# Merging two quarter-array products of an attention step into one of 64 rows and 128 columns

## The chip, the cores and the metric

The kernel runs on one core of one Trainium2 chip, in float32 throughout. The metric is the device time of one execution in microseconds (us), as the median of several runs. Beside it stands one profiled execution, from which every duration below is taken.

## The reference

x has the shape (2, 2048, 256). Four blocks follow one another, each adding its result to x after a layer norm: a gated linear scan, a feed-forward block with ternary weights, an attention of higher order, and the same feed-forward block again. The change lies in the attention. With 16 heads, 64 wide, q, k and v are projections of the normalised x, and per head, step by step in time:

```python
def step(carry, qkv):
    S_K, C_QV, G = carry
    q_t, k_t, v_t = qkv
    k_C = einsum('bhk,bhkv->bhv', k_t, C_QV)
    G = G + k_t[..., :, None] * k_C[..., None, :]
    S_K = S_K + k_t[..., :, None] * k_t[..., None, :]
    C_QV = C_QV + q_t[..., :, None] * v_t[..., None, :]
    S_C = einsum('bhkj,bhjv->bhkv', S_K, C_QV)
    o_t = einsum('bhk,bhkv->bhv', q_t, S_C - G)
    return (S_K, C_QV, G), o_t
...
out = outs.transpose(1, 0, 2, 3).reshape(b, t, H * DV) @ W_o
```

This is the same as two causal linear attentions in a row: u = sum over earlier and present k of k (k.q), and o = sum over earlier and present v of v (u.q).

## The kernel before

The kernel first runs the scan and the first feed-forward block ("front"), then the attention, into which the start of the second feed-forward block is woven, then the rest of that block. The order of the instructions on TensorE (PE), VectorE (DVE), ScalarE (ACT) and GpSimd (POOL) is written out by hand: what the code calls first comes first on its engine. SyncE (SP) issues the transfers, in order.

The attention has 32 steps, `s` = 0 to 31: 16 pieces of 128 rows in time, for each of the two batches in turn (even steps are called `first` in the code). A step's 128 rows are two chunks of 64, `c` = 0 and 1; the 16 heads are 8 pairs, `p`, and the two of a pair, `h`, lie in the two halves of the 128 partitions. So every product of the attention proper has 64 rows and 64 columns, and uses one quarter of TensorE's array. The weights are always the first operand, `lhsT`; the second, `rhs`, streams.

Per step, in the order of the instructions on TensorE:

- `inter(s, "S", "uT")` (line 1068) multiplies q with S, the sums of k kT over the earlier chunks, and leaves the result in two PSUM banks `huT`. In the first two steps, for which no earlier sums exist, it leaves out the half of c = 0.
- `products(s, "kT", "p1")` (L1051) multiplies q with k of its own chunk, into two banks `hp`; VectorE multiplies them with the causal mask into `p1` (L1057).
- `outward(s - 3, 1)` (L1129) is part of the output projection of an earlier step, five full-size products.
- `intra(s, "S", "kN", "p1", "uT")` (L1082) multiplies p1 with k and adds to the banks `huT`; `intra(s - 2, "M", ...)` (L1082) does the like for the second attention, with v.
- ScalarE evicts `huT` to `uT` in three copies (`evict`, L1093 and L1095).
- Then come projections of a later piece: q, k and v are each made by seven products (`Seven`, L992 and L997, banks `hqT_X` and so on), whose results ScalarE and VectorE copy and add.
- `update(s + 1, "kN", "kN", "S")` (L1108) adds the next step's k kT to the sums: VectorE writes S after each of its two chunks (L1118). `update(s - 1, "uN", "vN", "M")` is the like for the second attention, with sums M.
- `inter(s - 1, "M", "oT")` and `products(s - 1, "uT", "p2")` (L1068, L1051) are the second attention's products with q, and `outward(s - 2, 0)` starts the next output projection.

k is needed transposed (`kT`). This is done beside TensorE: VectorE transposes squares of 32 (`keys_out`, L235), SyncE writes them to memory and reads them back in another order into `rawkT` (`turn_rows`, four transfers), and ScalarE copies them into place (`turn_end`, L1148). `uN` is made from `uT` in the same way.

The eight PSUM banks are three rings: four banks `ps`, two `uT`, two `oT`. A bank is written again in turn, once what it held has been read. The product `hp` takes two `ps` banks, `huT` the two `uT` banks; the projections take `ps` for their bank Y, and `uT` or `oT` for X and Z.

Of the kernel before, what the change touches and what calls it, by code (L numbers as in the profile page):

```python
# [17 lines left out]
FP = mybir.dt.float32  # L18
AF = mybir.ActivationFunctionType
ALU = mybir.AluOpType  # L20
AX = mybir.AxisListType

P = 128
B, T, D = 2, 2048, 256
# [3 lines left out]
H, DK = 16, 64  # L28
NPR = H * DK // P
# [5 lines left out]
CH = 64  # L35
SQ = 32
NQ = P // SQ
# [6 lines left out]
def kernel(  # L44
# [15 lines left out]
    nc = tc.nc  # L60
# [7 lines left out]
    def bank(shape, name, tag="ps"):  # L68

        ring = rings[tag]  # L70
        ring.append(ring.pop(0))
        return psum_pool.tile(shape, FP, tag=f"bank{ring[-1]}", bufs=1, name=name)
# [67 lines left out]
    for c in range(2):  # L140
        r = slice(c * CH, (c + 1) * CH)
# [10 lines left out]
    def norm_stats(pool, cs, rms=False, bias=False, between=None):  # L152

        n, g0 = len(cs), cs[0]
        st = pool.tile([P, BC, 6], FP, tag="st", name=f"st{g0}")
        mv = pool.tile([P, BC, 2], FP, tag="mv", name=f"mv{g0}")
        rs = pool.tile([P, BC], FP, tag="rs", name=f"rs{g0}")
        for c, g in enumerate(cs):
            nc.vector.bn_stats(st[:, c, :], x_sb[:, g, :])  # L159
            nc.vector.bn_aggr(mv[:, c, :], st[:, c, :])  # L160
            if between and c == n // 2 - 1:
                between()
        mean, var = mv[:, :n, 0], mv[:, :n, 1]
        r = rs[:, :n]
        if rms:


            nc.vector.tensor_scalar(r, var, LN_EPS, RMS_EPS * RMS_EPS / D, ALU.add, ALU.mult)
            nc.vector.tensor_tensor(r, r, var, ALU.max)  # L169
        else:  # L170
            nc.gpsimd.tensor_scalar_add(r, var, LN_EPS)
        nc.gpsimd.tensor_tensor(r, r, mhalf[:, :n], ALU.pow)  # L172
        nb = None
        if bias:
            nb = pool.tile([P, BC], FP, tag="nb", name=f"nb{g0}")
            nc.gpsimd.tensor_tensor(nb[:, :n], mean, r, ALU.mult)
            nc.gpsimd.tensor_scalar_mul(nb[:, :n], nb[:, :n], -1.0)  # L177
        return mv, rs, nb
# [748 lines left out]
    def attention(keep, pool, state, last):  # L927
        halves = [slice(0, CH), slice(CH, P)]

        def feats(h, p):  # L930

            return slice(p * P + h * DK, p * P + (h + 1) * DK)
# [6 lines left out]
        def pair_sums(n):  # L939

            x = pairs[n]
            S = pool.tile([P, 4, P], FP, tag="S", bufs=1, name=f"S{n}")
            l, r = slice(0, P), slice(P, 2 * P)
            x11, x12, x21, x22 = x[:, 0, l], x[:, 1, l], x[:, 0, r], x[:, 1, r]
            for o, a, b_, op in (
                (S[:, 0, :], x21, x22, ALU.add), (S[:, 1, :], S[:, 0, :], x11, ALU.subtract),
                (S[:, 2, :], x11, x21, ALU.subtract), (S[:, 3, :], x12, S[:, 1, :], ALU.subtract),
            ):
                nc.gpsimd.tensor_tensor(o, a, b_, op)  # L949
            pairs[n] = x, S  # L950
# [89 lines left out]

        mask8 = mask2.unsqueeze(1).to_broadcast([P, NPR, CH])

        def products(s, left, nm):


            b, n = steps[s]
            banks = [bank([P, NPR, CH], f"h{nm}{b}_{n}_{h}") for h in range(2)]
            for p in range(NPR):
                for c in range(2):
                    for h in range(2):  # L1050
                        nc.tensor.matmul(  # L1051
                            banks[h][halves[c], p, :], lhsT=d[s][left][halves[h], p, halves[c]],
                            rhs=d[s]["qT"][halves[h], p, halves[c]], start=True, stop=True,
                        )
            d[s][nm] = pool.tile([P, 2, NPR, CH], FP, tag=nm, bufs=1, name=f"{nm}{b}_{n}")
            for h in range(2):
                nc.vector.tensor_tensor(d[s][nm][:, h], banks[h], mask8, ALU.mult)  # L1057

        def inter(s, sums, nm):

            b, n = steps[s]
            banks = [bank([P, NPR, CH], f"h{nm}{b}_{n}_{c}", nm) for c in range(2)]
            for p in range(NPR):
                for c in range(2):
                    if d[s][sums][c] is None:
                        continue
                    for h in range(2):
                        nc.tensor.matmul(  # L1068
                            banks[c][halves[h ^ c], p, :], lhsT=d[s][sums][c][halves[h], p, :],
                            rhs=d[s]["qT"][halves[h], p, halves[c]],  # L1070
                            start=(p == 0), stop=False, skip_group_check=True,
                        )
            d[s][nm + "b"] = banks

        def intra(s, sums, nat, pm, nm):

            b, n = steps[s]
            banks = d[s][nm + "b"]
            for p in range(NPR):
                for c in range(2):  # L1080
                    for h in range(2):
                        nc.tensor.matmul(  # L1082
                            banks[c][halves[h ^ c], p, :], lhsT=d[s][nat][halves[c], feats(h, p)],
                            rhs=d[s][pm][halves[c], h, p, :],
                            start=(d[s][sums][c] is None and p == 0), stop=True,
                            skip_group_check=True,
                        )

        def evict(s, nm, copy=act):
            b, n = steps[s]  # L1090
            banks = d[s][nm + "b"]
            t = pool.tile([P, NPR, P], FP, tag=nm, bufs=2 if nm == "uT" else 1, name=f"{nm}{b}_{n}")
            copy(t[:, :, halves[0]], banks[0])  # L1093
            for h in range(2):
                copy(t[halves[h], :, halves[1]], banks[1][halves[h ^ 1], :, :])  # L1095
            d[s][nm] = t

        def update(s, left, right, sums):


            b, n = steps[s]
            prev = before.get((b, sums))
            last = n == CPB - 1
            banks = [bank([P, NPR, DK], f"h{sums}{b}_{n}_{c}") for c in range(1 if last else 2)]
            for p in range(NPR):
                for c in range(len(banks)):
                    for h in range(2):
                        nc.tensor.matmul(  # L1108
                            banks[c][halves[h], p, :], lhsT=d[s][left][halves[c], feats(h, p)],
                            rhs=d[s][right][halves[c], feats(h, p)], start=True, stop=True,  # L1110
                        )
            d[s][sums] = [prev]
            for c in range(len(banks)):
                t = state.tile([P, NPR, DK], FP, tag=f"{sums}{b}", bufs=3, name=f"{sums}{b}_{n}_{c}")
                if prev is None:
                    nc.vector.tensor_copy(t, banks[c])
                else:
                    nc.vector.tensor_tensor(t, prev, banks[c], ALU.add)  # L1118
                d[s][sums].append(t)
                prev = t  # L1120
            before[b, sums] = prev
# [19 lines left out]
        def turn_rows(s, nm):  # L1141
            d[s]["r" + nm] = squares_in(pool, nm + "{}_{}".format(*steps[s]), d[s]["d" + nm], 2)

        def turn_end(s, nm):

            b, n = steps[s]
            t = pool.tile([P, NPR, P], FP, tag=nm, bufs=1, name=f"{nm}{b}_{n}")
            act(t, d[s]["r" + nm].rearrange("p t q -> p q t"))  # L1148
            d[s][nm] = t
# [18 lines left out]

        NS = len(steps)
        pair_sums(0)  # L1170
        stats = norm_stats(norm_pool, pair(1), bias=True)
        k, q, v = Seven(0, "kN", "oT"), Seven(0, "qT", "uT"), Seven(0, "vN", "oT")
        k.go(2, 1, 0, 5)
# [2 lines left out]
        q.go(1)  # L1176
        k.go(3)
        keys_out(0)
        turn_rows(0, "kT")
        k.go(7)  # L1180
        q.go(0, 5, 6)
        xn = norm_rows(norm_pool, pair(1), stats)
# [7 lines left out]
        q.go(4)  # L1190
        update(0, "kN", "kN", "S")
        v.go(6)
        turn_end(0, "kT")
        v.go(3, 7)
        for s in range(NS):
            first, n = s % 2 == 0, s // 2
            more = n + 1 < CPB
            inter(s, "S", "uT")
            products(s, "kT", "p1")
            if first and n + 2 < CPB:  # L1200
                stats = norm_stats(norm_pool, pair(n + 2), bias=True)
            elif s == NS - 4:
# [20 lines left out]
            last.part()  # L1223
            if s >= 3:
                outward(s - 3, 1)
            intra(s, "S", "kN", "p1", "uT")
            if s >= 2:
                intra(s - 2, "M", "vN", "p2", "oT")
            if s + 1 < NS:
                turn_rows(s + 1, "kT")  # L1230
            evict(s, "uT")
            if not more:
                evict(s - 2, "oT", act if first else dve)
                last.begin(first)
# [48 lines left out]
            if s == NS - 1:  # L1283
                update(s, "uN", "vN", "M")
            if first and not more:
                turn_end(s + 1, "kT")
            if not more:
                fill(2)
            elif first:
# [9 lines left out]
            if first and s > 0:  # L1299
                units_out(s)  # L1300
            if more:
                turn_end(s + 1, "kT")
            if s >= 1:
                inter(s - 1, "M", "oT")
                products(s - 1, "uT", "p2")
# [47 lines left out]
    def pair(n):  # L1353
        return [b * CPB + n for b in range(B)]
# [101 lines left out]
    with tc.tile_pool(name="keep", bufs=3) as keep_pool:  # L1456
# [10 lines left out]
        with tc.tile_pool(name="ffn2", bufs=1) as ffn_pool, tc.manual_schedule(engines=by_hand):  # L1467
            tags = ("uT", "ps", "oT")
            steps = last.outs
# [61 lines left out]
```

## Time and profile before

| | |
|---|---|
| time, median of 3 runs | 1206.71 us (1206.5 to 1206.82) |
| the profiled execution's own time | 1205.26 us |
| its span in the profile | 1203.4 us |
| TensorE matmuls busy | 1194.4 us |
| TensorE weight loads busy (they overlap the matmuls) | 972.1 us |
| VectorE busy | 816.0 us |
| ScalarE busy | 619.9 us |
| GpSimd busy | 252.5 us |
| steps of the attention in the span | from about 319 to about 1005 us |

The profile's page lists the busy time of each engine, the chain of waits that ended last, and the groups of instructions by line. The timeline gives instructions in order of time, neighbours of one kind merged to one line with a count. An f32 matrix product of the code appears as two weight loads and two matmuls; a matmul that reads f32 is thus counted twice. Groups of matmuls overlap in the timeline by the time that the last of a group takes to leave the array.

### The profile page before, as it was taken

How to read it: one execution, taken by the hardware profiler on the slowest of the kernel's cores; microseconds unless marked ns; L12 is line 12 of the kernel's file. 1: busy time of each engine (PE TensorE's matmuls, PEld its weight loads, DVE VectorE, ACT ScalarE, POOL GpSimd, SP SyncE). 2: the span in 40 equal slices, each digit the busy share in tenths (PEclk: the TensorE clock that was granted, in tenths of full speed). 3: DMA queues.
4: the chain of work that ended last, by engine and by line, in shares of the span. 5: the costliest groups of instructions: out<-in, count | busy, mean ns of one | idle time of the engine just before them, and what ended most of it. 6: DMA issues, size and time to landing. Idle time of an engine off the chain costs nothing.

```text
span 1203.4 us, 46653 instructions
## 1 busy us (share of the span) xinstructions
PE 1194.4 (99%) x21156; PEld 972.1 (81%) x21156; DVE 816.0 (68%) x1323; ACT 619.9 (52%) x983; POOL 252.5 (21%) x382
## 2 busy tenths in 40 slices
PE   9999999999999999999999999999999999999998
PEld 7599999999677777777777777777777889999998
DVE  7967877875667667666666756766666655677764
ACT  5366775543554554555545455455455452555442
POOL 3765235461110110110011011011001102222330
PEclk9999999999999999999999999999999999999999
DMA  9111111120244234234324323323433631212111
GB/s 336 71 62 36 36 36 35 37 71 1 89 130 138 92 108 125 91 108 142 117 84 133 125 84 125 126 92 107 130 105 101 183 100 46 71 71 71 54 53 36
DMA packets 80550, 112.99 MB, mean 94 GB/s; under 512 B 8288, under 2 KB 65504, under 8 KB 80096
## 3 DMA queue, kind: packets, MB, share of 16 engines
q1 hardware_dynamic: 77872, 106.07, 26.6%
q10 hardware_dynamic: 2448, 3.93, 1.1%
q8 instruction: 166, 2.72, 1.0%
q14 instruction: 32, 0.26, 0.1%
q0 software_dynamic: 32, 0.00, 0.0%
HBM read 58.59 MB, written 51.38 MB: 91 GB/s over the span
## 4 chain that ended last, share of the span: by engine, by line
PE 98%; DVE 1%; issue 0%; DMA 0%; ACT 0%; POOL 0%; ACTq 0%; DVEq 0%; POOLq 0%
PE hy L1129 10%; PE ox L632 10%; PE hx L539 9%; PE hkN_X L997 5%; PE hp L1051 5%; PE hqT_X L992 5%; PE hvN_X L997 5%; PE oz L632 5%; PE hz L539 5%; PE pq L339 3%; PE huT L1082 3%; PE hS L1108 3%; PE huT L1068 3%; PE hoT L1068 3%; PE hoT L1082 3%; PE hM L1108 3%
## 5 line engine op out<-in xcount | busy, mean ns | idle before, releaser
L1057 DVE TENSOR_TENSOR p<-hp,mask 128x512 f32<-128x512 f32 x128 | 82.1, 682 | 83.2 <-PE hp L1051 83.2
L949 POOL TENSOR_TENSOR S<-xnT 128x128 f32<-128x128 f32 x32 | 14.8, 463 | 531.4 <-ACT xnT L283 513.7
L1129 PE MATMUL hy<-wo,oT 128*128 128x256 f32 x512 | 123.7, 385 | 0.0
L191 ACT ACTIVATE xn<-x_sb,nb,rs 128x256 f32<-128x256 f32 x124 | 65.8, 592 | 85.4 <-POOL nb L177 83.5
L1129 PEld LDWEIGHTS hy<-wo,oT 128*128 128x128 f32 x512 | 93.6, 190 | 19.0 <-issue 6.7
L551 ACT ACTIVATE hT<-hT,b_sb 128x256 f32<-128x256 f32 x192 | 85.4, 501 | 34.6 <-DVE hT L583 31.7
L1093 ACT COPY uT<-huT 128x512 f32<-128x512 f32 x32 | 18.8, 586 | 129.3 <-PE huT L1082 129.3
L1118 DVE TENSOR_TENSOR S<-S,hS 128x512 f32<-128x512 f32 x60 | 41.2, 687 | 43.0 <-PE hS L1108 39.9
L235 DVE STREAM_TRANSPOSE sqkT<-kN 128x1024 f32<-128x1024 f32 x32 | 65.9, 2059 | 1.3 <-ACT kN L1028 1.2
L1148 ACT COPY kT<-rawkT 128x1024 f32<-128x1024 f32 x32 | 66.7, 2084 | 0.0
L235 DVE STREAM_TRANSPOSE squN<-uT 128x1024 f32<-128x1024 f32 x31 | 63.6, 2051 | 4.1 <-ACT uT L1095 3.7
L1148 ACT COPY uN<-rawuN 128x1024 f32<-128x1024 f32 x31 | 64.6, 2085 | 1.7 <-DMA rawuN<-dsquN 1.3
L516 POOL TENSOR_TENSOR xT<-xnT 128x256 f32<-128x256 f32 x15 | 16.9, 1124 | 179.2 <-ACT xnT L283 118.5
L159 DVE BATCH_NORM_STATS2 st<-x_sb 128x6 f32<-128x256 f32 x128 | 51.4, 403 | 2.3 <-DMA x_sb<-in_x_dram 2.3
L1108 PEld LDWEIGHTS hS<-kN 64*64 64x64 f32 x1984 | 32.7, 134 | 23.2 <-issue 23.1
L1002 DVE TENSOR_TENSOR kN<-kN,hkN_Y 128x512 f32<-128x512 f32 x16 | 11.0, 686 | 58.1 <-ACT kN L1011 58.1
L1028 ACT COPY vN<-hvN_X 128x512 f32<-128x512 f32 x16 | 9.4, 587 | 78.8 <-PE hvN_X L997 78.8
L172 POOL TENSOR_TENSOR rs<-rs,mhalf 128x2 f32<-128x2 f32 (+1 forms) x43 | 38.9, 904 | 33.1 <-DVE rs L169 30.3
L640 DVE TENSOR_TENSOR x_sb<-x_sb,ox 128x256 f32<-128x256 f32 x63 | 26.0, 413 | 28.8 <-PE ox L632 28.8
L622 DVE TENSOR_TENSOR hS<-hT 128x512 f32<-128x512 f32 x62 | 41.2, 686 | 5.6 <-ACT hT L551 5.6
L1118 DVE TENSOR_TENSOR M<-M,hM 128x512 f32<-128x512 f32 x60 | 41.0, 684 | 4.6 <-PE hM L1108 1.4
L1082 PEld LDWEIGHTS huT<-p,kN 64*64 64x64 f32 x2048 | 33.4, 134 | 12.8 <-issue 7.0
(303 smaller groups left out, 3031.1 us busy)
## 6 DMA issues: line engine op xcount, KB each, us to landing
dsqkT<-sqkT SPq DMA_DIRECT2D x32, 512.0 KB, 3.6
rawkT<-dsqkT SPq DMA_DIRECT2D x128, 128.0 KB, 3.0
dsquN<-squN SPq DMA_DIRECT2D x31, 512.0 KB, 3.4
rawuN<-dsquN SPq DMA_DIRECT2D x124, 128.0 KB, 3.1
out_dram<-x_sb SPq DMA_DIRECT2D x15, 256.0 KB, 2.2
x_sb<-in_x_dram SPq DMA_DIRECT2D x7, 512.0 KB, 8.9
dsqxn<-sqxn SPq DMA_DIRECT2D x14, 256.0 KB, 4.0
rawxn<-dsqxn SPq DMA_DIRECT2D x56, 64.0 KB, 2.4
```

The lines of the kernel that those rows point to most:

```text
L235: nc.vector.transpose(to, src)
L539: nc.tensor.matmul(at[a][:, j, :], lhsT=A[:, f * P : (f + 1) * P], rhs=Bm, start=(new and j == 0), stop=True, skip_group_check=True,)
L551: nc.scalar.activation(out, out if src is None else src[:, j, :], AF.Gelu, bias=b1_sb[:, f : f + 1])
L632: nc.tensor.matmul(banks[name][:, c, :], lhsT=A[f // 2][:, f % 2, c * P : (c + 1) * P], rhs=Bm[:, f, :], start=(new and c == 0 and f == 0) ...
L997: nc.tensor.matmul(to, lhsT=self.A[i], rhs=self.B[i], start=new, stop=True, skip_group_check=True)
L1057: nc.vector.tensor_tensor(d[s][nm][:, h], banks[h], mask8, ALU.mult)
L1068: nc.tensor.matmul(banks[c][halves[h ^ c], p, :], lhsT=d[s][sums][c][halves[h], p, :], rhs=d[s]["qT"][halves[h], p, halves[c]], start=(p = ...
L1082: nc.tensor.matmul(banks[c][halves[h ^ c], p, :], lhsT=d[s][nat][halves[c], feats(h, p)], rhs=d[s][pm][halves[c], h, p, :], start=(d[s][su ...
L1108: nc.tensor.matmul(banks[c][halves[h], p, :], lhsT=d[s][left][halves[c], feats(h, p)], rhs=d[s][right][halves[c], feats(h, p)], start=True ...
L1118: nc.vector.tensor_tensor(t, prev, banks[c], ALU.add)
L1129: nc.tensor.matmul(py, lhsT=d[s]["oT"][:, p, :], rhs=wo[:, p, :], start=(p == 0), stop=(p == NPR - 1),)
L1148: act(t, d[s]["r" + nm].rearrange("p t q -> p q t"))
```

## The change

The weights of `inter(s, "S", "uT")` and of `products(s, "kT", "p1")` are laid side by side in one tile `W`, of 9 slots with 2 times 64 columns: in each slot `W[:, p, 0]` holds kT and `W[:, p, 1]` holds S. A product takes 128 neighbouring columns of it. For the lower half of the partitions (h = 0) kT is shifted by one slot, so that its 128 columns are S and then k, and for h = 1 they are k and then S. `wide_products` is thus one product of 64 rows and 128 columns with q where there were two; its result has S q in one half of the partitions and k q in the other, in four banks (two of the ring `uT` for c = 0, two of `ps` for c = 1).

Around it:

- VectorE masks k q in four instructions on 64 partitions, where it had two on 128.
- `wide_intra` adds p1 times k to the half of each bank that holds S q. It now stands behind `intra(s - 2, "M", ...)`, not ahead of it.
- `wide_evict` copies the four half banks to `uT`, where there were three copies.
- `keys_in` reads the transposed k into a buffer with 8 more elements, one element further on for the lower half, and GpSimd clears one element at either end. `keys_end` copies it to the two tiles `W` (c = 0 and 1) in two ScalarE instructions of 9 x 64 elements, where there was one of 1024.
- `update` writes the sums S into `W`. The tiles of c = 0 have three buffers, those of c = 1 one. The sums M get one buffer for c = 0 and three for c = 1, for both batches, where there were three for each batch.
- For the first two steps the sums are set to zero and the products with them are computed.

```diff
+        def wide(c):
+            return state.tile([P, NPR + 1, 2, CH], FP, tag=f"W{c}", bufs=1 if c else 3, name=f"W{c}")
+
+        def wide_products(s):
+            b, n = steps[s]
+            banks = [[bank([P, NPR, CH], f"hu{b}_{n}_{h}{c}", "ps" if c else "uT") for c in range(2)] for h in range(2)]
+            for c in range(2):
+                w = d[s]["W"][c].rearrange("p a two e -> p (a two e)")
+                for p in range(NPR):
+                    for h in range(2):
+                        at = (2 * p + 1 - h) * CH
+                        nc.tensor.matmul(
+                            banks[h][c][:, p, :], lhsT=w[halves[h], at : at + 2 * CH],
+                            rhs=d[s]["qT"][halves[h], p, halves[c]],
+                            start=(p == 0), stop=False, skip_group_check=True,
+                        )
+            d[s]["p1"] = pool.tile([P, 2, NPR, CH], FP, tag="p1", bufs=1, name=f"p1{b}_{n}")
+            for c in range(2):
+                for h in range(2):
+                    other = halves[1 - h]
+                    nc.vector.tensor_tensor(
+                        d[s]["p1"][halves[c], h], banks[h][c][other], mask8[other], ALU.mult
+                    )
+            d[s]["ub"] = banks
+
+        def wide_intra(s):
+            for p in range(NPR):
+                for c in range(2):
+                    for h in range(2):
+                        nc.tensor.matmul(
+                            d[s]["ub"][h][c][halves[h], p, :], lhsT=d[s]["kN"][halves[c], feats(h, p)],
+                            rhs=d[s]["p1"][halves[c], h, p, :],
+                            start=False, stop=True, skip_group_check=True,
+                        )
+
+        def wide_evict(s):
+            b, n = steps[s]
+            t = pool.tile([P, NPR, P], FP, tag="uT", bufs=2, name=f"uT{b}_{n}")
+            for c in range(2):
+                for h in range(2):
+                    act(t[halves[h], :, halves[c]], d[s]["ub"][h][c][halves[h]])
+            d[s]["uT"] = t
+
+        def keys_in(s):
+            dr = d[s]["dkT"]
+            raw = pool.tile([P, NPR * P + 8], FP, tag="raw", bufs=2, name="rawkT{}_{}".format(*steps[s]))
+            nc.gpsimd.memset(raw[halves[0], :1], 0.0)
+            nc.gpsimd.memset(raw[halves[1], NPR * P : NPR * P + 1], 0.0)
+            for b in range(NQ):
+                at = 1 if b < NQ // 2 else 0
+                nc.sync.dma_start(
+                    out=raw[b * SQ : (b + 1) * SQ, at : at + NPR * P].rearrange("i (a c) -> i a c", a=NQ),
+                    in_=dr[:, :, b, :].rearrange("a i c -> i a c"),
+                )
+            d[s]["rkT"] = raw
+
+        def keys_end(s):
+            for c in range(2):
+                r = d[s]["rkT"][:, c * CH * NPR : (c + 1) * CH * NPR]
+                act(
+                    d[s]["W"][c][:, :, 0, :],
+                    bass.AP(tensor=r.tensor, offset=r.offset, ap=[list(r.ap[0]), [1, NPR + 1], [NPR, CH]]),
+                )
...
-                t = state.tile([P, NPR, DK], FP, tag=f"{sums}{b}", bufs=3, name=f"{sums}{b}_{n}_{c}")
+                if sums == "S":
+                    w = wide(1 - c)
+                    if c == 0:
+                        d[s]["W"].append(w)
+                    else:
+                        d[s + B]["W"] = [w]
+                    t = w[:, :NPR, 1, :]
+                else:
+                    t = state.tile([P, NPR, DK], FP, tag=f"M{c}", bufs=3 if c else 1, name=f"M{b}_{n}_{c}")
...
-            inter(s, "S", "uT")
-            products(s, "kT", "p1")
+            wide_products(s)
...
-            intra(s, "S", "kN", "p1", "uT")
             if s >= 2:
                 intra(s - 2, "M", "vN", "p2", "oT")
+            wide_intra(s)
             if s + 1 < NS:
-                turn_rows(s + 1, "kT")
-            evict(s, "uT")
+                keys_in(s + 1)
+            wide_evict(s)
...
-                turn_end(s + 1, "kT")
+                keys_end(s + 1)
```

More of the change, by code (lines that the diff above doesn't have):

```diff
@@ L1170, in attention @@
         pair_sums(0)
+        for s in range(B):
+            w = wide(0)
+            nc.gpsimd.memset(w[:, :NPR, 1, :], 0.0)
+            d[s]["W"] = [w]
         stats = norm_stats(norm_pool, pair(1), bias=True)
@@ L1178, in attention @@
         keys_out(0)
-        turn_rows(0, "kT")
+        keys_in(0)
         k.go(7)
@@ L1192, in attention @@
         v.go(6)
-        turn_end(0, "kT")
+        keys_end(0)
         v.go(3, 7)
@@ L1301, in attention @@
             if more:
-                turn_end(s + 1, "kT")
+                keys_end(s + 1)
             if s >= 1:
```

## The prediction

> **What bounds the kernel now.** I read the page first: the busy times, then the chain of waits. TensorE works in 99% of the span and carries 98% of the chain that ended last, at full clock; every other engine is far below.
>
> ```profile
> span 1203.4 us, 46653 instructions
> ...
> PE 1194.4 (99%) x21156; PEld 972.1 (81%) x21156; DVE 816.0 (68%) x1323; ACT 619.9 (52%) x983; POOL 252.5 (21%) x382
> ...
> PEclk9999999999999999999999999999999999999999
> ...
> PE 98%; DVE 1%; issue 0%; DMA 0%; ACT 0%; POOL 0%; ACTq 0%; DVEq 0%; POOLq 0%
> ```
>
> A busy PE row says only that some matmul was in flight, so what a matmul costs has to come from how often they start. For that I took the timeline of TensorE inside one step of the attention (columns: start, length, engine, line, operation, tiles, shapes, count). The length of a group includes the 0.22 us that its last instruction takes to drain; the distance between the starts of neighbouring groups is what counts.
>
> ```profile
> 724.00 1.05 PE L992 MATMUL hqT_X<-xnT,wq 128*128 128x128 f32 x8
> 724.89 1.02 PE L997 MATMUL hvN_X<-wv,xnT 128*128 128x512 f32 x2
> ...
> 739.03 1.46 PE L1129 MATMUL hy<-wo,oT 128*128 128x256 f32 x6
> 740.42 1.16 PE L1068 MATMUL huT<-qT,S 64*64 64x64 f32 x64
> 741.40 1.11 PE L1051 MATMUL hp<-qT,kT 64*64 64x64 f32 x64
> 742.45 2.43 PE L1129 MATMUL hy<-wo,oT 128*128 128x256 f32 x10
> ```
>
> The two groups that the change merges are L1068 huT (q with the sums) and L1051 hp (q with k). Each has 32 products in the code and 64 instructions here: an f32 product is two passes, each a weight load and a matmul. Both together occupy TensorE from 740.42 to 742.45, 2.03 us, nothing idle between them, in each of 32 steps.
>
> What sets their pace? One place in the trace runs the same kind of product on two quarters only: the last step, where an update makes only half its banks.
>
> ```profile
> 989.86 2.08 PE L1108 MATMUL hM<-vN,uN 64*64 64x64 f32 x64
> ```
>
> 64 instructions on two quarters: 2.08 - 0.22 = 1.86 us, 32 per quarter, 58 ns each. On four quarters: 1.16 - 0.22 = 0.94 us, 16 per quarter, 59 ns each. A quarter takes one pass every 58 to 59 ns whatever the others do; the number of instructions does not set the pace (14.7 ns apart on four quarters, 29 on two).
>
> Last, the groups by line with shapes kept apart (columns: busy us, mean ns of one).
>
> ```profile
> L1051 PE MATMUL hp<-qT,kT 64*64 64x64 f32 x2048 | 36.2, 218 | 0.2 <-issue 0.2
> ...
> L992 PE MATMUL hqT_X<-xnT,wq 128*128 128x128 f32 x128 | 16.9, 275 | 0.0
> ...
> L1051 PEld LDWEIGHTS hp<-qT,kT 64*64 64x64 f32 x2048 | 33.3, 135 | 0.4 <-issue 0.4
> ...
> L992 PEld LDWEIGHTS hqT_X<-xnT,wq_t 128*128 128x128 f32 x128 | 15.5, 191 | 1.6 <-DVE qT L1002 0.5
> ```
>
> A matmul lasts 57 ns longer for 64 more streamed columns (275 - 218), and a load 56 ns longer for 64 more weight columns (191 - 135): both run at about 0.88 ns a column. With 64 and 64 columns, load and stream are equally long and overlap (one pass in 58 ns); with 128 and 128 a pass takes (724.89 - 724.00) / 8 = 111 ns. So today's passes are balanced. Which of the two sets the pace cannot be seen in them, and the change tips the balance.
>
> **The change, part by part.** *The merged product.* It has 32 products of 64 rows, 128 weight columns and 64 streamed columns, 64 instructions, on two halves of the array: 32 passes per half. Each streams 64 columns as before, but loads 128. If the longer of the two sets the pace, a pass costs 111 ns: 32 x 111 = 3.55 us. Before, 2 x 0.94 = 1.88 us. That is +1.67 us a step, on the path, 32 steps: +53.5 us. The first two steps, whose huT has half its products, gain nothing from that: their two quarters take the same time, and the change computes the zero sums too. Bounds for a pass under this reading: 107 ns (128 x 0.83, the slope from 128 to 512 columns, (595 - 275) / 384) to 118 (twice 59): +1.5 to +1.9 us a step, +49 to +61 us. I take 111, the measured row.
>
> [...]
>
> The number of instructions halves. By the rows that is worth nothing: they start 14.7 ns apart on four quarters, and with half as many on two quarters the pace per quarter stays. [...]
>
> *Changes of array shape.* The neighbours of the merged group are full-size matmuls (L1129) as before, and the two products with p stay together. No shape change is added: 0.
>
> *Masks.* Two of 128x512 (L1057, 682 ns each, the pair in 1.29 us) become four of 64x512, which by L1095 on VectorE (two in 1.39 us) last as long: +1.3 us a step, +42 us on VectorE, 816 to 858 of some 1260. Their cover: the first pair can start when the c = 0 half of the product is done, 1.8 us before its end; then the outward part (2.4 us) and the product p2 with v (0.98 us), which the change puts ahead of the product p1 with k, run before p1 is read. The second pair ends 1.5 us after the product, 3.3 us are there. Nothing on the path from the third step on; in the first, without that cover, about 1 us.
>
> *Eviction of uT.* ScalarE's 0.59 + 1.17 us become four of 64x512, 2.34 us. The product p1 with k now comes last, so the eviction starts about 1 us later against what follows. The queued copies behind it shift by up to 1.5 us in odd steps: the copy of rawuN (2.05 us), then the first qT and vN copies, for whose banks the sixth products wait. In odd steps qT's first copy moves from 725.09 to about 726.7 and ends at 727.3; its bank is written again at 727.50. It fits by 0.2 us. In even steps the kN product after next wants the first uT bank, free about 0.7 us after the eviction can begin, with 0.96 us of L997 ahead of it. Without this cover it would cost its 0.6 us a step.
>
> *k's turn.* One ScalarE copy of 1024 elements (2.08 us) becomes two of 576 at the same stride, 2 x 1.17 us: +0.26 us. It ends at 712.7 in the even step that I followed (709.67 + 0.59 + 2.4), where q's product starts at 715.74, and in the odd one at 738.1 against 740.42. The merged product now needs both, where huT needed only the sums, but the margin stays above 2 us. The four rows of k's transfer land 4 bytes off; the first copy of them begins 4 us after they land (703.29 + 3.06 against 710.15): hidden. Two tiny writes on GpSimd now wait for the same buffer as the transfers, and ScalarE's two copies wait for them; what stands behind them on GpSimd, the sums of x, has the 37 us of idle that the timeline shows ahead of it at 740.94. SyncE's order is unchanged. M's first half with one buffer is read and rewritten a step apart, except in the last step: under 1 us.
>
> Waits altogether: I take 0.1 us a step, 3 us. Bounds: -1 (the 1.1 us idle at L1082 now) to +0.5 a step, 16 us, if the shifted copies on ScalarE miss their banks each time.
>
> Sum: +53.5 + 3 = +57 us. The profiled execution took 1205.26 us, span 1203.4 and 1.9 around it; it becomes 1262. The median of the runs is 1.45 above it: 1206.71 + 57 = 1264.
>
> **Rivals.**
>
> *The load keeps up (not slower).* A row half today receives 2 x 64 weight columns in one pass time, as two loads for two quarters side by side (the L1051 group). If one load of 128 columns for 64 rows is as fast, a pass stays at 58.5 ns, the product costs 32 x 58.5 = 1.87 us, and only waits are left: -1 to +16, about 1209. For it: that quarters are fed in parallel, and that the loads of the transposes (L215, 128 columns, one pass) last 141 ns. Against: in every two-pass product of the trace a load of 128 columns lasts 56 ns longer than one of 64. It decides below about 61 ns a pass: at 61, 32 x 2.5 x 32 is 2.6 us, no longer nothing.
>
> *Instructions bind (faster).* If the issue of small products were the limit, half of them would take 0.94 us for the 1.88: -0.94 x 32 = -30 us, 1177 us. Against: the 64 instructions on two quarters took twice as long as on four. It needs a pass in a half at 30 ns.
>
> *No overlap in a half (much slower).* If the two halves, which now share all output columns, cannot load side by side, 64 x 111 = 7.1 us: +5.2 a step, 1374 us. If a half could not load while it streams, 111 + 53 ns a pass: 1316 us. Against: L1051 has quarters above each other in turn and runs as fast as groups on the diagonal.
>
> *It doesn't do what it says:* products stay 64 columns wide. The instructions as built show 128, so I give it no chance of its own.
>
> **How the numbers follow.** Load sets the pace: 0.82; the load keeps up: 0.10; instructions bind: 0.04; no overlap: 0.04. The forecast's own ends are 49 - 1 = +48 and 61 + 16 = +77: 1254 to 1284. That holds nearly all of 0.82, and with it eight in ten; the three others lie outside. A measurement of this kernel tells a change of 0.2%, 2.4 us, from none. The rival at about 1209 splits: 0.01 faster, 0.05 same, 0.04 slower. Faster: 0.04 + 0.01 = 0.05; same 0.05; slower 0.82 + 0.04 + 0.04 = 0.90.
>
> **What would show it.** Right: the merged group's 64 instructions take about 3.6 us between the starts of their neighbours, loads of 64x128 last about 190 ns, and two start every 111 ns; L1068's other use and L1082 keep 0.94 to 0.98; TensorE stays at 99%. Wrong: a pass at 58 ns, or a load at 135; or idle TensorE ahead of the sixth products (qT, vN, kN) that adds up to more than 16 us.

## The result, and the profile after

| | before | after |
|---|---|---|
| median of five runs | 1206.71 us (1205.84 to 1207.13) | 1268.59 us (1262.36 to 1268.67) |
| profiled execution, its span | 1205.26, 1203.4 us | 1268.59, 1266.8 us |

The ratio is 1.0501, with a 95% interval of 1.0486 to 1.0515: 5% slower. The five runs after spread over 6 us, which those before do not. The mean granted TensorE clock goes with it: 0.994 in the three runs at 1268.6, 0.997 at 1264.91, 0.999 at 1262.36. That is the second finding below.

The page of the changed kernel: TensorE is as full as before, with 1984 matmuls fewer and 61 us more.

```profile
span 1266.8 us, 43085 instructions
...
PE 1255.5 (99%) x19172; PEld 1031.4 (81%) x19172; DVE 864.3 (68%) x1387; ACT 643.6 (51%) x1047; POOL 258.6 (20%) x448
...
PEclk9999999999899999999999999999999989999999
```

The timeline of TensorE in one step, the same stretch as was shown before:

```profile
964.81 1.46 PE L1209 MATMUL hy<-wo,oT 128*128 128x256 f32 x6
966.20 3.79 PE L1059 MATMUL hu<-qT,W 64*128 64x64 f32 x64
969.92 2.42 PE L1209 MATMUL hy<-wo,oT 128*128 128x256 f32 x10
```

64 instructions in place of 128, and 969.92 - 966.20 = 3.72 us from neighbour to neighbour in place of 2.03: +1.69 us in each of 32 steps, 54.1 us. Groups by line (busy us, mean ns of one):

```profile
L1059 PE MATMUL hu<-qT,W 64*128 64x64 f32 x2048 | 122.1, 275 | 1.4 <-ACT kN L1028 0.7 <-ACT qT L1028 0.7
L1059 PEld LDWEIGHTS hu<-qT,W 64*128 64x128 f32 x2048 | 117.6, 189 | 12.8 <-issue 9.3 <-ACT kN L1028 1.5 <-ACT qT L1028 0.9
```

A load of 64 rows and 128 columns takes 189 ns, as one of 128 rows and 128 columns did (190), where one of 64 rows and 64 columns took 135: halving the rows makes no difference here, halving the columns does. In the trace the starts in one half lie 111 to 112 ns apart, once the group has begun. A matmul that streams 64 columns is now listed with 275 ns, where it was 218. The profile models the ends of matmuls, so this length is not used here; the starts are.

### The profile page after: what moved, and what is told of

The parts are those of the page before. It is cut to its first block, busy times and chain, and to the rows that moved or that the text cites. A ratio compares the mean times of both kernels' runs of the same rounds, so it can differ in the third digit from the quotient of the medians.

```text
span 1266.8 us, 43085 instructions
## 1 busy us (share of the span) xinstructions
PE 1255.5 (99%) x19172; PEld 1031.4 (81%) x19172; DVE 864.3 (68%) x1387; ACT 643.6 (51%) x1047; POOL 258.6 (20%) x448
## 4 chain that ended last, share of the span: by engine, by line
PE 98%; DVE 1%; issue 0%; ACT 0%; POOL 0%; ACTq 0%; DVEq 0%; POOLq 0%
PE hu L1059 9%; PE hy L1209 9%; PE ox L632 9%; PE hx L539 9%; PE hkN_X L997 5%; PE hqT_X L992 5%; PE hvN_X L997 5%; PE oz L632 4%; PE hz L539 4%; PE pq L339 3%; PE hS L1179 3%; PE hoT L1153 3%; PE hoT L1139 3%; PE hM L1179 3%; PE hu L1078 2%; PE hp L1122 2%
## 5 line engine op out<-in xcount | busy, mean ns | idle before, releaser
L1089 ACT COPY uT<-hu 64x512 f32<-64x512 f32 x128 | 74.3, 580 | 214.4 <-PE hu L1078 212.1
L1068 DVE TENSOR_TENSOR p<-hu,mask 64x512 f32<-64x512 f32 x128 | 88.2, 689 | 73.3 <-PE hu L1059 71.3
L1059 PEld LDWEIGHTS hu<-qT,W 64*128 64x128 f32 x2048 | 117.6, 189 | 12.8 <-issue 9.3
L1059 PE MATMUL hu<-qT,W 64*128 64x64 f32 x2048 | 122.1, 275 | 1.4 <-ACT kN L1028 0.7
L1109 ACT COPY W<-rawkT 128x576 f32<-128x576 f32 x64 | 77.0, 1254 | 0.0
L1198 DVE TENSOR_TENSOR W<-W,hS 128x512 f32<-128x512 f32 x60 | 41.3, 688 | 32.5 <-PE hS L1179 29.3
L1128 DVE TENSOR_TENSOR p<-hp,mask 128x512 f32<-128x512 f32 x64 | 40.9, 680 | 20.3 <-PE hp L1122 20.3
```

Of the source, the lines that this page charges most:

```text
L1059: nc.tensor.matmul(banks[h][c][:, p, :], lhsT=w[halves[h], at : at + 2 * CH], rhs=d[s]["qT"][halves[h], p, halves[c]], start=(p == 0), sto ...
L1068: nc.vector.tensor_tensor(d[s]["p1"][halves[c], h], banks[h][c][other], mask8[other], ALU.mult)
L1089: act(t[halves[h], :, halves[c]], d[s]["ub"][h][c][halves[h]])
L1109: act(d[s]["W"][c][:, :, 0, :], bass.AP(tensor=r.tensor, offset=r.offset, ap=[list(r.ap[0]), [1, NPR + 1], [NPR, CH]]),)
```

## The experiments

Distances between the first products with q of successive steps show where each kernel spends its time, from the profiled execution of each (us; odd and even are the usual values of the middle steps):

| kernel | odd | even | step 0 | step 1 | step 30 |
|---|---|---|---|---|---|
| before | 24.68 | 18.44 | 13.03 | 21.20 | 19.79 |
| after | 26.38 | 20.28 | 15.81 | 26.09 | 25.55 |
| e1_quarters | 24.68 | 18.58 | 14.70 | 21.26 | 24.01 |
| e4_waits | 26.38 | 20.27 | 18.12 | 23.87 | 20.64 |
| e5_waits | 26.38 | 20.28 | 15.06 | 23.87 | 20.64 |
| e6_quarters_order | 24.68 | 18.44 | 14.69 | 21.25 | 19.78 |

In the middle the changed kernel is 1.70 us longer in odd steps and 1.84 in even ones. Steps 0, 1 and 30 carry more, and those are the ones in which TensorE stood idle or its clock fell (a fall costs its step 3.4 us, as is worked out at e4_waits).

**e1_quarters: everything but the merged product.**

```diff
-nc.tensor.matmul(banks[h][c][:, p, :], lhsT=w[halves[h], at : at + 2 * CH], ...)
+for j in range(2):
+    nc.tensor.matmul(banks[h][c][halves[j], p, :],
+                     lhsT=w[halves[h], at + j * CH : at + (j + 1) * CH], ...)
```

> The changed kernel with each merged product split again into two of 64 weight columns, on the two quarters side by side; all the rest of the change (tiles W, four masks, four evictions, two copies of k, the order) stays. Theory (the loads of 128 columns set the pace): the group goes from 3.72 us back to about 2.0 us, so 32 x 1.7 = 54 us less than the changed kernel's 1262 to 1269; 1208 to 1215 us, what is left over 1206.7 being waits and clock dips. Rival (the rest of the change, its masks, evictions and order, carries a large part of the loss): 1225 us or more.

Measured: 1213.4 us (1213.19 to 1216.18), ratio 1.0064 (1.0049 to 1.0079) to 1206.11 of the kernel before beside it. The group is back at 2.02 us:

```profile
745.94 2.09 PE L1060 MATMUL hu<-qT,W 64*64 64x64 f32 x128
747.96 2.42 PE L1210 MATMUL hy<-wo,oT 128*128 128x256 f32 x10
```

Its middle odd steps are those of before and its even ones 0.14 us longer. So the merged product alone makes 1.70 us in every middle step, 54.4 us for 32 of them.

The times differ by less. At the same mean clock of 0.999 the changed kernel took 1262.36 us and e1_quarters 1213.2: 49.2 us. The profiled executions show where the other 5 us are. Five middle steps of e1_quarters (8, 10, 14, 16 and 23) are 0.2 to 1.1 us longer than the usual ones, 3.2 us together; the trace names no reason, and the changed kernel has one such step, of 0.15 us. (The kernel before has four, 11, 24, 25 and 26, 1.7 us together.) In steps 0, 1, 2 and 29 the difference between the two, without the fall of the clock in step 1, is below 1.70 us, by 2.1 us in all. So the 7 us that e1_quarters takes over the kernel before are not what the rest of the change costs in the changed kernel. At clock 0.999 that one is 1262.36 - 1206.71 = 55.7 us longer in all, only 1.3 us more than the 54.4.

**e2_stream128: twice the stream under the same load.**

```diff
-banks[h][c][:, p, :], ..., rhs=d[s]["qT"][halves[h], p, halves[c]],
+two neighbouring slots of banks[h][c], ..., rhs=d[s]["qT"][halves[h], p, :],
```

> The changed kernel with 128 columns of q streamed in each merged product in place of 64 (the sums it makes are not those of the reference). Theory: a load of 128 columns takes as long as a stream of 128, both overlap, a pass stays at 111 ns and the time at 1262 to 1269 us. Rival (in a half, load and stream do not overlap, 64 streamed columns are part of the 111 ns): 53 ns more for each of 1024 passes of a half, 1317 us or more. On the clock: if the half-empty stream is what lets the clock drop, the dips at the start of the attention go away; if idle time alone does, they stay.

Measured: 1266.05 us (1263.89 to 1267.03), ratio 1.0489 (1.0472 to 1.0507). The timeline's group:

```profile
730.58 3.84 PE L1060 MATMUL hu<-qT,W 64*128 64x128 f32 x64
734.35 2.43 PE L1210 MATMUL hy<-wo,oT 128*128 128x256 f32 x10
```

3.77 us against 3.72: twice as many streamed columns for 0.05 us, which go at the start of the group; within it the starts lie 111 to 112 ns apart as before. Stream and load overlap in a half, and in the changed kernel half of the stream's time was empty.

The median is below the changed kernel's 1268.59 because the clock fell less: its mean is 0.997 to 1.0 in these four runs, where three of the changed kernel's five have 0.994. In the profiled run the fall at the start of the attention is gone, that at step 30 is not. That is the first of the two cases that were set down for the clock, though in few runs.

**e3_cols96: fewer columns to load, in the same shape of tile.**

```diff
-banks[h][c][:, p, :], lhsT=w[halves[h], at : at + 2 * CH],
+banks[h][c][:m, p, :], lhsT=w[halves[h], at : at + m],      # m = 128 for p = 0, else 96
...
-d[s]["p1"][halves[c], h], banks[h][c][other], mask8[other], ALU.mult
+d[s]["p1"][halves[c], h], banks[h][c][halves[0]], mask8[halves[0]], ALU.mult
```

> The changed kernel with 96 weight columns in place of 128 in 28 of the 32 merged products of a step (the result is not that of the reference). Theory: a pass goes with its loaded columns, 96 x 0.83 + 5 = 85 ns, 26 ns less for 28 of 32 passes of a half in 32 steps: 23.5 us less than the changed kernel, 1239 to 1245 us. Rival (the shape of the tile, all 128 output columns in use, sets the pace): no difference, 1262 to 1269 us.

Measured: 1238.65 us (1238.45 to 1241.49), ratio 1.0274 (1.0258 to 1.0289). Timeline and loads:

```profile
736.05 3.04 PE L1060 MATMUL hu<-qT,W 64*128 64x64 f32 x64
739.02 2.43 PE L1210 MATMUL hy<-wo,oT 128*128 128x256 f32 x10
```

```profile
L1060 PEld LDWEIGHTS hu<-qT,W 64*96 64x96 f32 x1792 | 81.5, 162 | 0.0
```

The group takes 2.97 us, the starts in a half lie 85 ns apart where 96 columns are loaded, and the whole is 23.7 us less than the changed kernel's 1262.36 (the run at clock 0.999, as the three lower ones here), 0.35 us under the expected range. A pass follows the columns of its load: 58, 85 and 112 ns for 64, 96 and 128. A matmul here multiplies with just the columns that its load brings, 96 too, so no run tells the load itself from the use of as many columns; what is shown is that the weight columns set the pace and, by e2_stream128, the streamed ones do not.

**e7_swapped: the wide operand streams.**

```diff
-lhsT=w[halves[h], at : at + 2 * CH], rhs=d[s]["qT"][halves[h], p, halves[c]]      # two halves
+lhsT=d[s]["qT"][halves[h], p, halves[c]], rhs=w[c][halves[h], at : at + 2 * CH]   # four quarters
```

> e1_quarters with the merged product turned round: the 64 columns of q are the weights, the 128 columns of S and k stream, 32 products on the four quarters (the sums come out turned and later steps use them as they lie, so the result is not that of the reference). Theory (a pass costs the longer of load and stream; 0.83 ns a column plus 5 ns; quarters run side by side): 16 passes of 111 ns per quarter, 1.78 us, about 1.95 us between the neighbours' starts against 2.02 in e1_quarters and 3.72 in the changed kernel; 1210 to 1213 us. Rival (the halving of the instructions helps once the load is short): 1.0 us, 1180 us.

Measured: 1209.01 us (1207.23 to 1211.98), ratio 1.0027 (1.0018 to 1.0037), 1 us under the theory's 1210 to 1213.

```profile
742.60 1.98 PE L1059 MATMUL hu<-W,qT 64*64 64x128 f32 x64
744.50 2.43 PE L1209 MATMUL hy<-wo,oT 128*128 128x256 f32 x10
```

The same 64 instructions as in the changed kernel, with the two operands exchanged, take 1.90 us in place of 3.72: a pass of 110 ns, now set by the stream, but on four quarters. Against e1_quarters, with twice as many instructions, it is 0.12 us less. In this group the number of instructions is not the limit.

**e4_waits and e5_waits: the idle time and the clock.** The timeline of the changed kernel at step 30, and the busy times around it and around step 1 (columns: window, its length, then PE, PEld, DVE, ACT, POOL, granted clock, DMA share, GB/s):

```profile
1021.83 2.38 ACT L1089 COPY uT<-hu 64x512 f32<-64x512 f32 x4 [6.72 <-PE hu L1078]
...
1023.57 1.03 PE L539 MATMUL hz<-xT_last,w_s_back 128*128 128x256 f32 x4
...
1024.22 0.59 ACT L1164 COPY oT<-hoT 128x512 f32<-128x512 f32 x1
1024.82 1.17 ACT L1166 COPY oT<-hoT 64x512 f32<-64x512 f32 x2
...
1026.01 0.59 ACT L557 COPY hT<-hx 128x512 f32<-128x512 f32 x1
...
1026.70 1.75 PE L539 MATMUL hx<-xT_last,w_s_back 128*128 128x256 f32 x4 [2.10 <-issue]
```

```profile
337.50:344.00 6.50, 6.50 (x66) 4.88 (x67) 4.10 (x4) 0.00 (x0) 0.00 (x0) 0.50 0.06 21
...
1024.60:1026.70 2.10, 0.00 (x1) 0.03 (x1) 0.07 (x1) 1.95 (x4) 0.00 (x0) 1.00 0.00 0
1027.00:1033.80 6.80, 6.80 (x104) 5.64 (x103) 2.98 (x5) 3.67 (x5) 0.00 (x0) 0.50 0.13 41
```

The feed-forward product hx wants its bank back, whose copy (L557) stands on ScalarE behind the four copies of uT and three of oT: TensorE is idle for 2.1 us. Right after it the clock is 0.50 for 6.83 us by the trace's record. The same four matmuls of the feed-forward (`hx<-xT_last,w_back`) take 1.86 us to the next start inside that stretch (1031.99) and 0.97 after it, at clock 1.00 (1036.83), so the fall costs about half of its length, 3.4 us. The like happens at 337.5, again for 6.83 us, after a wait of 0.68 us ahead of step 1's merged product:

```profile
334.75 4.61 PE L1059 MATMUL hu<-qT,W 64*128 64x64 f32 x64 [0.68 <-ACT kN L1028]
```

There, c = 0 of the zero sums, which the kernel before left out, needs a bank that ScalarE is still copying.

```diff
-for c in range(2):
+for c in (1, 0) if s < B else (0, 1):        # e4_waits; e5_waits: if s == 1
...
-evict(s - 2, "oT", act if first else dve)
+evict(s - 2, "oT", dve)
```

> The changed kernel with its two longest waits of TensorE taken away: in the first two steps the products of the second chunk come first, so that the bank that ScalarE still reads is needed 1.8 us later; in the last but one step VectorE in place of ScalarE evicts oT, whose two copies held up the feed-forward block by 2.1 us. Theory: the waits (0.7 + 2.1 us) and the two stretches at half clock that follow them (3.4 us each) go: 1259 to 1261 us in every run, clock 1.0. Rival (the clock drops for the merged group itself, which streams only half the time): the dips stay, times between 1260 and 1266 us.

Measured: 1263.45 us (1262.9 to 1265.53), ratio 1.0477 (1.0461 to 1.0493): a miss of the expected 1259 to 1261. Step 30 is mended (20.64 for 25.55), but in step 0 the second half of W, which ScalarE writes last, was now wanted first; TensorE waited for it, and the clock fell to 0.50 at 322.7:

```profile
320.03 4.74 PE L1059 MATMUL hu<-qT,W 64*128 64x64 f32 x64 [1.14 <-ACT W L1109]
```

> As e4_waits, but the second chunk comes first only in step 1; in step 0, where it made TensorE wait 1.1 us for the second half of W, the order is the changed kernel's. Theory (idle TensorE time of a microsecond or two lets the clock drop; the merged group itself does not): no dip near 323, 337 or 1027 us, the waits of 0.7 us at step 1 and 2.1 us at step 30 gone, 1259 to 1261 us in all runs. Rival (the half-empty stream of the merged group brings the dips about): dips at the start of the attention stay in some runs, 1263 us or more there.

Measured: 1261.41 us (1260.71 to 1261.73), ratio 1.0457 (1.0442 to 1.0473), the median 0.4 us above the expected range. The clock is 0.999 or 1.0 in all four runs and the spread 1 us. So the merged group by itself, 32 times in each run, did not bring the clock down. The 0.7 us wait by itself did not either in the profiled runs of e1, e2 and e3, which have it in step 1 without a fall there; they fell at step 30 only, where all three keep an idle time of 2.0 to 2.1 us. In these three the stream of the group is fuller than in the changed kernel. Whether the half-empty stream helps a short wait to bring the clock down at step 1, the few runs cannot settle.

The waits themselves were worth about 1 us, not the 2.8 that were expected (1261.41 against 1262.36). Step 30 is 1.5 us shorter, the fall of the clock left out. The 0.7 us of step 1 came back elsewhere: with the second chunk first, p1's product waits for VectorE's masks (0.4 us of idle TensorE), and steps 0 and 1 together take 38.93 us, against 38.83 in e2_stream128, which has the changed kernel's order and no fall there.

**e6_quarters_order: the eviction early again.**

```diff
 # e1_quarters, and:
-intra(s - 2, "M", "vN", "p2", "oT")
-wide_intra(s)
+wide_intra(s)
+intra(s - 2, "M", "vN", "p2", "oT")
```

> e1_quarters with the product of p1 with k put back ahead of the product of p2 with v, as before the change, so that the eviction of uT can begin 1 us earlier. Theory (the new order and the longer eviction make the 0.14 us by which even steps are longer than before): even steps 18.44 us again, 2 to 3 us less than e1_quarters' 1213.2. Rival (the four masks are late for p1 in this order): TensorE waits for VectorE at the product of p1 with k, even steps longer than 18.58, 1214 us or more.

Measured: 1209.79 us (1209.09 to 1211.7), ratio 1.0033 (1.0022 to 1.0044). That is 3.4 us less than e1_quarters' undisturbed 1213.2, a little more than expected; step 30 gained too (19.78 us, against 20.6 without the fall of the clock). Nine of the thirteen even steps from 4 to 28 are 18.44 again, so the 0.14 us belong to the new order with the longer eviction; the other four, 10 to 16, are 18.7 to 18.8. The loads of p1's product now wait 11 us in all for VectorE's masks, which is the rival's mechanism, though nearly all of it is hidden under matmuls still in flight: TensorE itself is idle for 0.4 us by it. In the changed kernel the 0.14 us are here:

```profile
743.52 0.59 ACT L1011 COPY kN<-hkN_X 128x512 f32<-128x512 f32 x1
...
743.79 1.16 PE L1179 MATMUL hS<-kN 64*64 64x64 f32 x64
...
744.14 0.69 DVE L1002 TENSOR_TENSOR kN<-kN,hkN_Y 128x512 f32<-128x512 f32 x1 [4.42 <-ACT kN L1011]
...
744.77 1.26 PE L1179 MATMUL hM<-vN,uN 64*64 64x64 f32 x64
```

The copy of kN starts right behind the eviction of uT; VectorE's addition of bank Y follows it and ends at 744.83, and the second bank of hM is, by the order of the ring, bank Y. hM lasts 1.26 us in place of 1.11 in the kernel before:

```profile
707.46 1.11 PE L1108 MATMUL hM<-vN,uN 64*64 64x64 f32 x64
```

In e6_quarters_order, where the copy of kN comes earlier, it is 1.11 again.

None of these versions beats the kernel before.

## Why the prediction was right

The median of 1268.59 lies in 1254 to 1284; the forecast was 1264. The mechanism was right: the columns of the longer load set the pace. The sum has no term for falls of the clock, and 6 us of the median are theirs (1268.59 against 1262.36). That it lies in the range all the same is owed to the range's width, which was meant for other waits. By its steps, for the profiled execution (+63.3 us):

- *The merged product:* +53.5 forecast, from the pass of 111 ns of a full-size load. Measured 111 to 112 ns a pass, 54.1 us from the groups and 54.4 from the middle steps against e1_quarters. The weight columns as the limit are shown twice, by e3 (96 columns, 85 ns) and e2 (a longer stream costs 0.05 us a group). The rows made no difference to the load (189 ns for 64 against 190 for 128), and the pass grows by 27 ns for each 32 columns loaded (58, 85, 112). A whole pass is 4 to 5 ns above the 107 of the lower bound, 128 columns at the 0.83 ns of the trace before, which would have given 49 us.
- *The rivals:* "the load keeps up" is refuted by the pass of 112 ns, where it needed 58, and by e3; "instructions bind" by that pass too and by e7, where half the instructions save 0.12 us and not 1 us, and "no overlap" by e2 for a half and by the pass of 112 ns on both halves at once. Why the loads of the transposes, which spoke for the first rival, last only 141 ns stays open.
- *Masks:* four take 2.75 us for 1.29 on VectorE and cost nothing in the middle steps of the changed order; odd steps are 24.68 in e1, to the hundredth. VectorE's busy time grew by 48 us, where 42 were worked out.
- *Eviction:* the copies of qT in odd steps fitted, as worked out (in the step that begins at 753.19 the first ends at 766.48, and its bank is written again at 766.65). In even steps the price was 0.14 us at a bank that the working did not follow (Y, by way of the copy of kN), about the 0.1 that was taken for waits.
- *What was mis-sized:* without the product and the falls of the clock 2.4 us are left (63.3 - 54.1 - 6.8), near the 3 us that were taken for waits. That is partly luck: the middle even steps alone make 0.14 x 14 = 2.0 us, the ends add to it, and the 1.7 us of irregular delays that the kernel before has are gone. Step 30, where ScalarE also evicts oT and copies the feed-forward's X, was not followed: 2.1 us idle. And a wait was priced at its own length, where it cost 3.4 us more by the clock at half speed that came behind it, twice in the profiled execution: 6.8 us, which the sum took at nothing. The falls of the clock make the spread of the runs; the run without them, 1262.36, is 1.6 us under the forecast.

## What to carry to other kernels

Where the weights of a small product change every time, a pass went here with the longer of its load and its stream, each by its columns: 58 ns for 64 loaded and 64 streamed, 85 for 96 and 64, 112 for 128 and 64, 112 for 128 and 128, 110 for 64 and 128. Widening the shorter of the two was nearly free (e2_stream128); widening the load doubled the pass on half as many tiles. Before merging two products with a common operand, ask which of the two operands is common. Here it streamed, so no load was spared. Where it was the load (e7_swapped), the group kept four quarters and gained 0.12 us, too little to show in the time. A count of instructions says nothing of this: compare start to start on two and on four tiles first.

## What was not expected of the hardware

One idle stretch of TensorE of 2.1 us, in a stream that was full before and after, was followed by 6.83 us at a granted clock of 0.50 in the changed kernel. In e4_waits one of 1.14 us was, ahead of the merged group, while one of 1.16 us in the profiled execution of e6_quarters_order, ahead of full-size matmuls, was not. In the profiled execution of e7_swapped an idle time of 2.1 us was followed by 3.41 us at 0.50, half as long. By the clock's record of the changed kernel, each stretch at one clock within the span, from its rise at the start to its last change, is a whole number of 3.413 us: 331.09, 6.83, 682.67, 6.83 and 232.11 us are 97, 2, 200, 2 and 68 of them. In both cases with a short idle time, step 1 of the changed kernel (0.68 us) and step 0 of e4_waits (1.14 us), the 3.413 us ahead of the fall hold nothing but that idle time and the merged group with its half-empty stream. That speaks for the stream counting too, but no run was made to show it.
